# Third cross attention of a decoder: the folded weights' products in row halves of TensorE

## The chip, the cores and the metric

The kernel runs on one core of one Trainium2 chip, in one launch. The metric is device time in microseconds (us), the median of several executions. The profile is of one execution.

## The reference

A decoder of four layers, each with a self attention, a cross attention and a feed-forward part, each followed by a layer norm over 256 features: `x = layernorm(x + part(x))`. x is 8 sequences of 56 tokens, 448 tokens in all; the context has 8 x 1500 rows of 64 features. All is float32. The change is in the cross attention of layer 3, which is, cut to what matters:

```python
# 16 heads H, K = 128, D_CQ = 192, R = 64, D_C = 64
q_hk  = (hidden_q @ Wq.T).reshape(b, s, 16, 128)          # Wq: (2048, 256)
q_big = einsum('bshk,hkq->bshq', q_hk, w_kc_q)            # w_kc_q: (16, 128, 192)
kv_rope = rope(kv_c)
q_r = einsum('bshq,hqr->bhsr', q_big, W_qr)               # W_qr: (16, 192, 64)
k_r = einsum('bld,hdr->bhlr', kv_rope, W_kr)              # W_kr: (16, 64, 64)
scores = einsum('bhsr,bhlr->bhsl', q_r, k_r)
attn = softmax(scores)
ctx_c = einsum('bhsl,bld->bhsd', attn, kv_rope)           # then w_kc_kv and Wo
```

In this layer no rotation stands between q_hk and the scores (layers 0 and 2 have one on q_big), so all weights in front of the scores can be multiplied into one matrix for each head: scores = x . m3(h) . kv_rope, where m3 has 256 x 64 elements.

## The kernel before

The steps of `STEPS` run one after the other: self attention, cross attention and feed-forward of the four layers. `load` brings the weights of the next step in while a step runs: it issues DMAs on SyncE's queue (SP) into a pool of 16 buffers of 128 x 1024 elements, so a load starts when a buffer comes free. `xattn(3)` has two stages.

The first makes the folded weights and the queries. For each head, in this order:

- wqk = W_qr . W_kr, 192 x 64 (lines 691 to 702). The 192 rows are two parts ("halves") of 96. A matmul contracts over R = 64, so the even head of a pair uses rows 0 to 63 of TensorE's array and the odd head rows 64 to 127. These 32 matmuls go to the tile `ps_wqk`, one for each half, and are copied to SBUF by ScalarE (half 0) and VectorE (half 1).
- `turn_x` transposes the normed x to xT, 8 transposes into `ps_xT` and one copy by ScalarE.
- m2 = w_kc_q . wqk, 128 x 64 (lines 738 to 745): two matmuls of 96 rows for each head, added in `ps_m2`, and one copy of 128 x 1024 by VectorE.
- m3 = Wq . m2, two blocks c of 128 x 64 (lines 746 to 751): one matmul of 128 rows for each head and block into `ps_m3`, and one copy for each block, c = 0 by ScalarE and c = 1 by VectorE.
- qa = m3 . xT (`pair`, lines 718 to 732): the two heads of a pair go to the two halves of the columns of the array, ScalarE copies them from `ps_qk` to `qa`, and after each four heads two DMAs on ScalarE's queue copy qa to the other half of the partitions. `rows_of` issues the first context rows on the same queue.

PSUM is cut into two buffers of two banks (`bank2`: ps_wqk, ps_xT, ps_m2 and ps_m3 take them in turn) and three of one bank (`bank`: ps_qk). Profile rows leave the digit of a name out, so ps_m is ps_m2 and ps_m3, and m is m2 and m3; they tell apart by their inputs (l3x_c holds w_kc_q, l3x_q holds Wq, l3x_r and l3x_k hold W_qr and W_kr).

The second stage (`x_tiles`) walks over 56 tiles of queries with an order of instructions written out by hand: scores, exponent, transposes, weighted sum. It begins when qa is there.

Ahead of the stage the last token tile of the layer norm is finished on VectorE and ScalarE: `add` (lines 438 to 443), `rsqrt` (407 to 412) and `norm` (449). A scheduler orders the instructions of each engine where the code doesn't fix it; `self.mm(..., fixed=True)` and `self.ordered` fix it.

The matmuls of m2 in the code before:

```python
self.mm(
    ps[:, h // 8, (h % 8) * DC : (h % 8 + 1) * DC],
    [(kcq[h // 4][:, half, h % 4, :], wqk(half, h)) for half in range(2)],
)
```

Of the kernel before, what the change touches and what calls it, by code (L numbers as in the profile page):

```python
# [9 lines left out]
F32 = mybir.dt.float32  # L10
# [7 lines left out]
NB, S, D = 8, 56, 256  # L18
T = NB * S
TT = 112  # L20
NT = T // TT
L, DC = 1500, 64
# [98 lines left out]
def _rows(a):  # L121

    n = a.shape[0] // 128
    return a.reshape(n, 128, -1).transpose(1, 0, 2).reshape(128, -1)
# [14 lines left out]
def _groups(a, n):  # L139

    k, m = a.shape[0] // 128, a.shape[1]
    return a.reshape(k, 128, m // n, n).transpose(1, 2, 0, 3).reshape(128, -1)


def _pack(i):
    w = {}
# [4 lines left out]
    p = "L0_attn_"  # L151
# [6 lines left out]
    for n in (0, 2, 3):  # L158
        p = f"L{n}_xattn_"
        if n == 3:  # L160
            w[f"l{n}x_q"] = _rows(i[p + "Wq"])
            kcq = i[p + "w_kc_q"].transpose(2, 0, 1).reshape(2, 96, 4, 4 * 128)
            w[f"l{n}x_c"] = kcq.transpose(1, 2, 0, 3).reshape(96, -1)
        else:
            w[f"l{n}x_q"] = _groups(i[p + "Wq"].T, 512)
            w[f"l{n}x_c"] = i[p + "w_kc_q"].transpose(1, 0, 2).reshape(128, -1)

        for k, a in (("r", i[p + "W_qr"]), ("k", i[p + "W_kr"])):
            w[f"l{n}x_{k}"] = a.reshape(8, 2, -1, 64).transpose(1, 3, 0, 2).reshape(128, -1)
        w[f"l{n}x_o"] = _rows(i[p + "Wo"].T)  # L170
        w[f"l{n}x_v"] = i[p + "w_kc_kv"].transpose(1, 0, 2).reshape(128, -1)

    p = "L0_ffn_"
# [6 lines left out]
    p = "L1_attn_"  # L180
# [6 lines left out]
    p = "L1_xattn_"  # L187
# [5 lines left out]
    p = "L1_ffn_"  # L193
# [8 lines left out]
    p = "L2_attn_"  # L202
    q, kv = i[p + "q_w"], i[p + "kv_w"]
    k = np.repeat(kv[:64].reshape(4, 1, 16, D), 4, axis=1).reshape(D, D)
# [7 lines left out]
    p = "L2_ffn_"  # L212
# [8 lines left out]
    p = "L3_attn_"  # L221
# [15 lines left out]
    p = "L3_ffn_"  # L237
# [17 lines left out]
class Decoder:  # L255
# [420 lines left out]
    def xattn(self, n):  # L676
        nc, tc = self.nc, self.tc
        qrT, krT = self.rowsets(f"l{n}x_r", 192), self.rowsets(f"l{n}x_k", DC)
        kckv, wo = self.rowsets(f"l{n}x_v", DC), self.rowsets(f"l{n}x_o", D)

        with tc.tile_pool(name="xa", bufs=1) as outer:


            wm = outer.tile([128, 8, D], F32, name="wm")


            qa = outer.tile([128, NB * NQ], F32, name="qa")
            with tc.tile_pool(name="xq", bufs=2) as pool, self.psum(2, 3):

                wqk = pool.tile([128, 2, 16, DC], F32, bufs=1, name="wqk")  # L690
                at = lambda half, h: wqk[:96, half, h % 2 * 8 + h // 2]
                for half in range(2):
                    ps = self.bank2("ps_wqk")
                    for h in range(16):
                        j, rows = h // 2, slice(h % 2 * DC, (h % 2 + 1) * DC)
                        self.mm(
                            ps[:96, h % 2, j * DC : (j + 1) * DC],
                            [(qrT(j)[rows, half * 96 : (half + 1) * 96], krT(j)[rows])], fixed=True,
                        )
                    (nc.vector.tensor_copy if half else nc.scalar.copy)(  # L700
                        wqk[:96, half].rearrange("p (u h) d -> p u (h d)", u=2), ps[:96]
                    )
                self.turn_x(range(NT))
                context = self.x_context(outer)
                self.x_queries(n, pool, at, qa, context[2])
            with tc.tile_pool(name="xs", bufs=1) as pool, tc.tile_pool(name="psx", bufs=1, space=PSUM) as banks:
                self.x_tiles(pool, banks.tile([128, 8, 512], F32, name="ps_x"), qa, wm, kckv, wo, *context)

    def x_queries(self, n, pool, wqk, qa, rows_of):
        nc, xT = self.nc, self.xT  # L710

        def by_batch(a):
            return a.rearrange("p (b s) -> p b s", b=NB)

        flat = qa.rearrange("p (b o n) -> p b o n", b=NB, o=2)

        def pair(h, terms_of):


            ps = self.bank("ps_qk")  # L720
            terms = [terms_of(h + odd) for odd in range(2)]
            for k in range(2):
                for odd in range(2):
                    self.ordered(nc.tensor.matmul, ps[odd * DC : (odd + 1) * DC, :T], *terms[odd][k], start=k == 0, stop=k == 1)
            for odd in range(2):
                rows = slice(odd * DC, (odd + 1) * DC)
                nc.scalar.copy(flat[rows, :, odd, h // 2 * S : (h // 2 + 1) * S], by_batch(ps[rows, :T]))  # L727
            if h % 4 == 2:
                cols = slice((h // 2 - 1) * S, (h // 2 + 1) * S)
                for odd in range(2):  # L730
                    rows, others = (slice(u * DC, (u + 1) * DC) for u in (odd, 1 - odd))
                    nc.scalar.dma_start(flat[others, :, odd, cols], flat[rows, :, odd, cols])

        if n == 3:
            wq = self.rowsets(f"l{n}x_q", 256)
            kcq = [a.rearrange("p (q h k) -> p q h k", q=2, h=4) for a in self.parts(f"l{n}x_c")]

            m2 = pool.tile([128, 16, DC], F32, bufs=1, name="m2")
            ps = self.bank2("ps_m2")
            for h in range(16):  # L740
                self.mm(
                    ps[:, h // 8, (h % 8) * DC : (h % 8 + 1) * DC],
                    [(kcq[h // 4][:, half, h % 4, :], wqk(half, h)) for half in range(2)],
                )
            nc.vector.tensor_copy(m2.rearrange("p (u h) d -> p u (h d)", u=2), ps)
            m3 = pool.tile([128, 2, 16, DC], F32, bufs=1, name="m3")
            for c in range(2):
                ps = self.bank2("ps_m3")
                for h in range(16):
                    self.mm(ps[:, h // 8, (h % 8) * DC : (h % 8 + 1) * DC], [(wq(h)[:, c * 128 : (c + 1) * 128], m2[:, h, :])])  # L750
                (nc.vector.tensor_copy if c else nc.scalar.copy)(m3[:, c].rearrange("p (u h) d -> p u (h d)", u=2), ps)
            for h in range(0, 16, 2):
                if h and h % 4 == 0:
                    rows_of(0, h // 4 - 1)
                pair(h, lambda h: [(m3[:, c, h], xT[:, c, :]) for c in range(2)])
            return

        wq, kcq = self.heads(f"l{n}x_q"), self.rowsets(f"l{n}x_c", 192)

        def table(name):  # L760
            return self.const(name).rearrange("p (a s) -> p a s", a=2).unsqueeze(2).to_broadcast([96, 2, NB, S])

        cos, sin = table("xq_cos"), table("xq_sin")

        heads, ropes = {}, {}

        def projected(h):
            ps = self.bank("ps_qh")
            self.mm(ps[:, :T], [(wq(c, h), xT[:, c, :]) for c in range(2)], fixed=True)
            qh = heads[h] = pool.tile([128, T], F32, name="qh")  # L770
            nc.scalar.copy(qh, ps[:, :T])

        def rotated(h):
            qh = heads.pop(h)
            big = self.bank2("ps_big")
            for half in range(2):
                self.mm(big[:96, half, :T], [(kcq(h)[:, half * 96 : (half + 1) * 96], qh)], fixed=True)
            view = big[:96, :, :T].rearrange("p a (b s) -> p a b s", b=NB)
            rope = ropes[h] = pool.tile([96, 2, T], F32, bufs=5, name="rope")
            turn = pool.tile([96, 2, T], F32, name="turn")  # L780
            nc.vector.tensor_tensor(rope.rearrange("p a (b s) -> p a b s", b=NB), view, cos, ALU.mult)  # L781
            nc.vector.tensor_tensor(turn.rearrange("p a (b s) -> p a b s", b=NB), view, sin, ALU.mult)  # L782
            for half in range(2):
                nc.gpsimd.tensor_tensor(rope[:, half, :], rope[:, half, :], turn[:, 1 - half, :], ALU.add)  # L784


        for h in range(-3, 16):
            if h + 3 < 16:
                projected(h + 3)
            if 0 <= h + 2 < 16:  # L790
                rotated(h + 2)
            if h >= 0 and h % 2:
                if h % 4 == 3 and h < 12:
                    rows_of(0, h // 4)
                pair(h - 1, lambda h: [(wqk(half, h), ropes[h][:, half, :]) for half in range(2)])

    def x_context(self, pool):

# [1021 lines left out]
```

## Time and profile before

| what | value |
| --- | --- |
| median of 3 runs | 1674.08 us (1666.78 to 1682.12) |
| the profiled execution's own time | 1675.49 us |
| its span, first to last instruction | 1673.2 us |
| mean granted clock of TensorE | 0.922 |
| TensorE weight loads (PEld), busy | 904.6 us (54% of the span) |
| VectorE (DVE) busy | 1092.4 us (65%) |
| ScalarE (ACT) busy | 623.7 us (37%) |
| first stage of the third cross attention | from 1319.7 us (first wqk matmul) to 1372 us (last qa DMA issued) |
| in it: first matmul of m2, of m3, of qa | 1324.06, 1335.74, 1349.56 us |
| first qa DMA issued | 1354.55 us |

Times inside an execution are counted from the span's start. A row of the profile names the line, the engine, the operation, the tile written and the tiles read, the shape, and how often; for a matmul the shape is rows * columns of the stationary operand, then rows x columns of the moving one. PE is TensorE's multiplication, PEld its weight load, which overlaps it. One float32 matmul of the code shows as two records. The granted clock is the share of TensorE's clock that was allowed in a stretch. The chain of waits is followed back from the last instruction to what released each step; a time without a releaser is called issue.

### The profile page before, as it was taken

Reading aid. Unit: us, or ns where it says so; the run is one execution under the profiler, and the core shown is the slowest. Engines: PE = TensorE matmul, PEld = TensorE weight load, DVE = VectorE, ACT = ScalarE, POOL = GpSimd, SP = SyncE. Lnnn points to the kernel's source line nnn. Section 1 sums busy time; section 2 is a strip of 40 time slices with the busy share of each in tenths; the row PEclk is TensorE's granted clock in tenths of the full one; section 3 lists DMA queues with packets and bytes.
Section 4 is the critical chain, followed back from the end, with each engine's and each line's share of the span. In section 5 each row is a group of like instructions: output and inputs, shape, how many; then the busy total and the mean of one; then the engine's idle time right before and its main releaser. Section 6 shows DMA issues by size and latency. Waiting matters only on the chain.

```text
span 1673.2 us, 37625 instructions
## 1 busy us (share of the span) xinstructions
PE 1507.2 (90%) x16308; PEld 904.6 (54%) x16308; DVE 1092.4 (65%) x1787; ACT 623.7 (37%) x910; POOL 323.6 (19%) x302
## 2 busy tenths in 40 slices
PE   7989979999878678998979999899987988999998
PEld 4666435556544344654435556665655844555646
DVE  0575579999576764336579999436463219999743
ACT  2431245655212332103245556222443034665420
POOL 4711511212122010021511212101121000221200
PEclk9999979999997888999979999797997877999999
DMA  9523422323020001222422322012210452232100
GB/s 357 189 76 113 122 59 77 103 78 84 23 95 13 27 26 43 70 79 77 120 74 81 99 84 78 24 60 73 64 58 20 145 132 61 79 87 84 53 1 11
DMA packets 52103, 133.74 MB, mean 80 GB/s; under 512 B 20689, under 2 KB 21153, under 8 KB 51938
## 3 DMA queue, kind: packets, MB, share of 16 engines
q1 hardware_dynamic: 19922, 65.36, 12.0%
q10 hardware_dynamic: 28368, 50.25, 10.7%
q0 software_dynamic: 3648, 15.73, 2.9%
q8 instruction: 128, 2.10, 0.5%
q14 instruction: 37, 0.30, 0.1%
HBM read 119.06 MB, written 6.75 MB: 75 GB/s over the span
## 4 chain that ended last, share of the span: by engine, by line
PE 51%; DVE 9%; issue 7%; ACT 2%; DMA 1%; POOL 1%; ACTq 1%; DVEq 0%; POOLq 0%
PE ps_x L366 17%; PE ps_glu L358 8%; PE ps_y L358 7%; PE ps_qk L1628 2%; DVE sc L366 2%; PE ps_v L1628 2%; PE ps_qh L358 2%; PE ps_m L358 1%; PE ps_big L358 1%; PE ps_y L1628 1%; PE ps_q L358 1%; PE ps_qk L366 1%; PE ps_low L358 1%; PE ps_s L1350 1%; DVE E L1371 1%
## 5 line engine op out<-in xcount | busy, mean ns | idle before, releaser
L366 PE MATMUL ps_x<-kvT,qa 64*128 64x375 f32 x1344 | 308.1, 562 | 30.9 <-DVE sc L366 24.6
L366 ACT ACTIVATE sc<-sc,tops 128x1500 f32<-128x1500 f32 x168 | 259.2, 1543 | 150.1 <-DVE sc L366 115.6
L366 DVE STREAM_TRANSPOSE eT<-sc 128x1536 f32<-128x1536 f32 x168 | 296.9, 1767 | 11.5 <-PE ps_x L366 8.2
L366 PE MATMUL ps_x<-eT,kv 32*64 32x224 f32 x9024 | 256.5, 356 | 4.2 <-issue 3.9
L366 PEld LDWEIGHTS ps_x<-eT,kv 32*64 32x64 f32 x9024 | 196.8, 132 | 70.2 <-issue 60.4
L366 PEld LDWEIGHTS ps_x<-kvT,qa 64*128 64x128 f32 x1344 | 113.1, 199 | 187.7 <-DVE sc L366 161.5
L366 DVE TENSOR_SCALAR_CACHE_REDUCE sc<-ps_x 128x750 f32<-128x750 f32 x168 | 157.3, 936 | 38.9 <-PE ps_x L366 38.9
L366 DVE TENSOR_SCALAR_CACHE_REDUCE sc<-ps_x,tops 128x750 f32<-128x750 f32 x168 | 161.0, 958 | 1.2 <-PE ps_x L366 0.8
L366 POOL TENSOR_TENSOR eT<-eyes,sums 128x224 f32<-128x224 f32 x24 | 13.3, 554 | 452.2 <-DVE sums L366 452.2
L784 POOL TENSOR_TENSOR rope<-rope,turn 96x448 f32<-96x448 f32 x64 | 70.9, 1129 | 65.0 <-DVE turn L782 65.0
L781 DVE TENSOR_TENSOR rope<-ps_big,consts 96x896 f32<-96x896 f32 x32 | 34.8, 1086 | 58.4 <-PE ps_big L358 58.4
L1144 ACT ACTIVATE act<-ps_glu 128x448 f32<-128x448 f32 (+1 forms) x52 | 28.2, 543 | 111.1 <-PE ps_glu L358 107.8
L1148 DVE TENSOR_TENSOR act<-ps_glu,act 128x448 f32<-128x448 f32 x43 | 26.8, 624 | 65.2 <-ACT act L1144 65.1
L408 ACT ACTIVATE rstd<-rstd 112x3 f32<-112x3 f32 (+2 forms) x21 | 4.3, 204 | 166.5 <-DVE rstd L407 166.4
L614 DVE RECIPROCAL rec<-rec 128x896 f32<-128x896 f32 x8 | 46.0, 5753 | 26.7 <-ACT rec L613 26.7
L440 DVE TENSOR_TENSOR X<-X,ps_y 112x256 f32<-112x256 f32 x32 | 13.5, 421 | 70.6 <-PE ps_y L358 70.6
L366 PE MATMUL ps_x<-wm,qa 128*112 128x128 f32 (+1 forms) x336 | 49.0, 302 | 9.6 <-DVE qa L366 9.6
L1695 POOL TENSOR_TENSOR qk<-qk,sw 128x896 f32<-128x896 f32 x16 | 33.3, 2080 | 105.4 <-DVE sw L1694 105.4
L366 PEld LDWEIGHTS ps_x<-wm,qa 128*112 128x112 f32 x336 | 42.3, 182 | 20.1 <-issue 11.2
L727 ACT COPY qa<-ps_qk 64x448 f32<-64x448 f32 x48 | 25.3, 526 | 67.7 <-PE ps_qk L366 53.8
L366 POOL TENSOR_TENSOR qa<-num,rec 64x448 f32<-64x448 f32 x42 | 47.9, 1139 | 2.9
L1692 DVE TENSOR_TENSOR qk<-ps_qk,consts 128x896 f32<-128x896 f32 x16 | 17.5, 1092 | 33.4 <-ACT sw L1689 16.8
(411 smaller groups left out, 2447.3 us busy)
## 6 DMA issues: line engine op xcount, KB each, us to landing
kv<-kv ACTq DMA_DIRECT2D x288, 128.0 KB, 2.7
kvT<-kvT POOLq DMA_DIRECT2D x24, 384.0 KB, 3.6
qa<-qa ACTq DMA_DIRECT2D x24, 224.0 KB, 3.6
raw<-in_ctx ACTq DMA_DIRECT2D x6, 512.0 KB, 4.1
kv<-raw POOLq DMA_DIRECT2D x6, 512.0 KB, 4.0
kvT<-by POOLq DMA_DIRECT2D x6, 512.0 KB, 4.4
l0a_q<-in_l0a_q SPq DMA_DIRECT2D x4, 512.0 KB, 11.0
l0a_c<-in_l0a_c SPq DMA_DIRECT2D x4, 512.0 KB, 8.7
```

The lines of the kernel that those rows point to most:

```text
L358: ins = self.nc.tensor.matmul(out, lhsT, rhs, start=n == 0, stop=n == len(terms) - 1)
L366: call(*args, **kw)
L614: nc.vector.reciprocal(rec, rec)
L727: nc.scalar.copy(flat[rows, :, odd, h // 2 * S : (h // 2 + 1) * S], by_batch(ps[rows, :T]))
L781: nc.vector.tensor_tensor(rope.rearrange("p a (b s) -> p a b s", b=NB), view, cos, ALU.mult)
L784: nc.gpsimd.tensor_tensor(rope[:, half, :], rope[:, half, :], turn[:, 1 - half, :], ALU.add)
L1144: nc.scalar.activation(act, ps[:m, 0, :T], AF.Silu)
L1148: nc.vector.tensor_tensor(act, ps[:m, 1, :T], act, ALU.mult)
L1350: tc.keep_in_program_order(nc.tensor.matmul(*args, **kw))
L1628: tc.keep_in_program_order(nc.tensor.matmul(*args, **kw))
L1692: nc.vector.tensor_tensor(view(qk), view(ps[:, :, :T]), cos4, ALU.mult)
L1695: nc.gpsimd.tensor_tensor(qk, qk, sw, ALU.add)
```

## The change

Only the third cross attention changes; layers 0 and 2 keep their code (moved into `x_weights`, and `pair` into `pair_of`).

- The 192 rows of wqk become three parts of 64. A matmul is 64 rows by 64 columns, the even head in rows and columns 0 to 63 of the array and the odd head in 64 to 127: 48 matmuls, three `ps_wqk` tiles. wqk holds the even heads in partitions 0 to 63 and the odd ones in 64 to 127.
- m2 contracts over 64 rows, three times for each head, even and odd heads in turn in the two row halves, each to its own bank: 48 matmuls in two groups of four head pairs, each with its own `ps_m2`.
- m3 contracts over two 64 row blocks k of m2 for each head and c, even and odd heads in turn: 64 matmuls, two groups of four head pairs. A group has both blocks c.
- Every group is copied by ScalarE (even heads) and VectorE (odd heads): 6 copies of 64 x 512 for wqk (2 of 96 x 1024 before), 8 of 64 x 256 for m2 (1 of 128 x 1024), 4 of 128 x 512 for m3 (2 of 128 x 1024).
- m2 and m3 are in an order fixed by `ordered`. The arrays of w_kc_q and Wq come in another layout from the host: l3x_c is 3 tiles of 128 x 1024 instead of 4 of 96 x 1024, l3x_q stays 4 tiles.

```diff
-            w[f"l{n}x_q"] = _rows(i[p + "Wq"])
-            kcq = i[p + "w_kc_q"].transpose(2, 0, 1).reshape(2, 96, 4, 4 * 128)
-            w[f"l{n}x_c"] = kcq.transpose(1, 2, 0, 3).reshape(96, -1)
+            q = i[p + "Wq"].reshape(8, 2, 2, 64, D)
+            w[f"l{n}x_q"] = q.transpose(1, 3, 0, 2, 4).reshape(128, -1)
+            kcq = i[p + "w_kc_q"].reshape(8, 2, 128, 3, 64)
+            w[f"l{n}x_c"] = kcq.transpose(1, 4, 3, 0, 2).reshape(128, -1)
...
+    def x_weights3(self, pool, qrT, krT):
+        wqk = pool.tile([128, 3, 8, DC], F32, bufs=1, name="wqk")
+        for part in range(3):
+            ps = self.bank2("ps_wqk")
+            for j in range(8):
+                for odd in range(2):
+                    rows = slice(odd * DC, (odd + 1) * DC)
+                    self.mm(
+                        ps[rows, odd, j * DC : (j + 1) * DC],
+                        [(qrT(j)[rows, part * DC : (part + 1) * DC], krT(j)[rows])], fixed=True,
+                    )
+            self.by_parity(lambda rows, odd: (wqk[rows, part].rearrange("p j d -> p (j d)"), ps[rows, odd]))
+        return wqk
+
+    def by_parity(self, copy):
+        for odd, call in enumerate((self.nc.scalar.copy, self.nc.vector.tensor_copy)):
+            call(*copy(slice(odd * DC, (odd + 1) * DC), odd))
...
+    def x_queries3(self, n, pool, wqk, qa, rows_of):
...
+        m2 = pool.tile([128, 2, 8, DC], F32, bufs=1, name="m2")
+        for four in range(2):
+            ps = self.bank2("ps_m2")[:, :, : 4 * DC].rearrange("p u (j d) -> p u j d", d=DC)
+            for j in range(4 * four, 4 * four + 4):
+                for part in range(3):
+                    for odd, rows in enumerate(halves):
+                        self.ordered(
+                            self.nc.tensor.matmul, ps[:, odd, j % 4], kcq[part][rows, j, :], wqk[rows, part, j],
+                            start=part == 0, stop=part == 2,
+                        )
+            for k in range(2):
+                self.by_parity(lambda rows, odd: (m2[rows, k, 4 * four : 4 * four + 4], ps[halves[k], odd]))
+        m3 = pool.tile([128, 2, 8, 2, DC], F32, bufs=1, name="m3")
+        for four in range(2):
+            ps = self.bank2("ps_m3").rearrange("p u (j c d) -> p u j c d", c=2, d=DC)
+            for j in range(4 * four, 4 * four + 4):
+                for c in range(2):
+                    for k in range(2):
+                        for odd, rows in enumerate(halves):
+                            self.ordered(
+                                self.nc.tensor.matmul, ps[:, odd, j % 4, c],
+                                wq[j // 2][rows, j % 2, k, c * 128 : (c + 1) * 128], m2[rows, k, j],
+                                start=k == 0, stop=k == 1,
+                            )
+            self.by_parity(lambda rows, odd: (m3[:, odd, 4 * four : 4 * four + 4], ps[:, odd]))
```

More of the change, by code (lines that the diff above doesn't have):

```diff
@@ L688, in xattn @@
             with tc.tile_pool(name="xq", bufs=2) as pool, self.psum(2, 3):
[L690 to L702, printed above, removed]
+                rotary = n != 3
@@ L703, in xattn @@
+                wqk = (self.x_weights if rotary else self.x_weights3)(pool, qrT, krT)
                 self.turn_x(range(NT))
                 context = self.x_context(outer)
-                self.x_queries(n, pool, at, qa, context[2])
+                (self.x_queries if rotary else self.x_queries3)(n, pool, wqk, qa, context[2])
             with tc.tile_pool(name="xs", bufs=1) as pool, tc.tile_pool(name="psx", bufs=1, space=PSUM) as banks:
                 self.x_tiles(pool, banks.tile([128, 8, 512], F32, name="ps_x"), qa, wm, kckv, wo, *context)
-    def x_queries(self, n, pool, wqk, qa, rows_of):
[L710 to L756, printed above, removed]
@@ new lines, in x_weights @@
+    def x_weights(self, pool, qrT, krT):
+        nc = self.nc
+        wqk = pool.tile([128, 2, 16, DC], F32, bufs=1, name="wqk")
+        for half in range(2):
+            ps = self.bank2("ps_wqk")
+            for h in range(16):
+                j, rows = h // 2, slice(h % 2 * DC, (h % 2 + 1) * DC)
+                self.mm(
+                    ps[:96, h % 2, j * DC : (j + 1) * DC],
+                    [(qrT(j)[rows, half * 96 : (half + 1) * 96], krT(j)[rows])], fixed=True,
+                )
+            (nc.vector.tensor_copy if half else nc.scalar.copy)(
+                wqk[:96, half].rearrange("p (u h) d -> p u (h d)", u=2), ps[:96]
+            )
+        return lambda half, h: wqk[:96, half, h % 2 * 8 + h // 2]
@@ new lines, in x_weights3 @@
+    def x_weights3(self, pool, qrT, krT):
+        wqk = pool.tile([128, 3, 8, DC], F32, bufs=1, name="wqk")
+        for part in range(3):
+            ps = self.bank2("ps_wqk")
+            for j in range(8):
+                for odd in range(2):
+                    rows = slice(odd * DC, (odd + 1) * DC)
+                    self.mm(
+                        ps[rows, odd, j * DC : (j + 1) * DC],
[3 more added lines that the diff above has]
+        return wqk
@@ new lines, in by_parity, with pair_of @@
+    def by_parity(self, copy):
+        for odd, call in enumerate((self.nc.scalar.copy, self.nc.vector.tensor_copy)):
+            call(*copy(slice(odd * DC, (odd + 1) * DC), odd))
+    def pair_of(self, ps, qa, h, terms):
+        nc = self.nc
+        flat = qa.rearrange("p (b o n) -> p b o n", b=NB, o=2)
+        for k in range(2):
+            for odd in range(2):
+                self.ordered(nc.tensor.matmul, ps[odd * DC : (odd + 1) * DC, :T], *terms[odd][k], start=k == 0, stop=k == 1)
+        for odd in range(2):
+            rows = slice(odd * DC, (odd + 1) * DC)
+            nc.scalar.copy(flat[rows, :, odd, h // 2 * S : (h // 2 + 1) * S], ps[rows, :T].rearrange("p (b s) -> p b s", b=NB))
+        if h % 4 == 2:
+            cols = slice((h // 2 - 1) * S, (h // 2 + 1) * S)
+            for odd in range(2):
+                rows, others = (slice(u * DC, (u + 1) * DC) for u in (odd, 1 - odd))
+                nc.scalar.dma_start(flat[others, :, odd, cols], flat[rows, :, odd, cols])
@@ new lines, in x_queries3 @@
+    def x_queries3(self, n, pool, wqk, qa, rows_of):
+        xT = self.xT
+        kcq = [a.rearrange("p (j k) -> p j k", j=8) for a in self.parts(f"l{n}x_c")]
+        wq = [a.rearrange("p (j k m) -> p j k m", j=2, k=2) for a in self.parts(f"l{n}x_q")]
+        halves = [slice(odd * DC, (odd + 1) * DC) for odd in range(2)]
+        m2 = pool.tile([128, 2, 8, DC], F32, bufs=1, name="m2")
[7 more added lines that the diff above has]
+                            start=part == 0, stop=part == 2,
+                        )
+            for k in range(2):
[5 more added lines that the diff above has]
+                for c in range(2):
+                    for k in range(2):
+                        for odd, rows in enumerate(halves):
[3 more added lines that the diff above has]
+                                start=k == 0, stop=k == 1,
+                            )
+            self.by_parity(lambda rows, odd: (m3[:, odd, 4 * four : 4 * four + 4], ps[:, odd]))
+        for h in range(0, 16, 2):
+            if h and h % 4 == 0:
+                rows_of(0, h // 4 - 1)
+            self.pair_of(self.bank("ps_qk"), qa, h, [[(m3[:, odd, h // 2, c], xT[:, c, :]) for c in range(2)] for odd in range(2)])
@@ L758, in x_queries @@
+    def x_queries(self, n, pool, wqk, qa, rows_of):
+        xT, nc = self.xT, self.nc
         wq, kcq = self.heads(f"l{n}x_q"), self.rowsets(f"l{n}x_c", 192)
@@ L794, in x_queries @@
                     rows_of(0, h // 4)
-                pair(h - 1, lambda h: [(wqk(half, h), ropes[h][:, half, :]) for half in range(2)])
+                self.pair_of(
+                    self.bank("ps_qk"), qa, h - 1,
+                    [[(wqk(half, g), ropes[g][:, half, :]) for half in range(2)] for g in (h - 1, h)],
+                )
     def x_context(self, pool):
```

## The prediction

> **What bounds the kernel now.** I read the page first: TensorE is busy for most of the span, so an edit of matmuls can count, but only where they stand on the chain.
>
> ```profile
> PE 1507.2 (90%) x16308; PEld 904.6 (54%) x16308; DVE 1092.4 (65%) x1787; ACT 623.7 (37%) x910; POOL 323.6 (19%) x302
> ```
>
> Then the chain of waits in order of time, from 1300 to 1370 us (start, us, what):
>
> ```profile
> 1319.80 2.89 PE ps_wqk L358 x64
> ...
> 1322.78 1.23 DVE wqk L700
> 1324.02 0.04 issue
> 1324.06 10.32 PE ps_m L358 x64
> 1334.38 1.36 issue
> 1335.74 13.89 PE ps_m L358 x64
> 1349.63 4.34 PE ps_qk L366 x16
> ```
>
> The stage's three products stand end to end, nothing beside them. wqk costs 2.9 us, m2 10.3, m3 13.9, and 1.4 pass between m2 and m3 in the copy of m2. Next the instructions that touch ps_m and ps_wqk (duration min/median/max; the form is rows*columns of the stationary part, then rows x streamed columns):
>
> ```profile
> L358 PE MATMUL ps_m<-wqk,l3x_c x64: 275/275/421, 1324.1 to 1334.0; 96*128 96x64 f32 x64
> L358 PE MATMUL ps_m<-m,l3x_q x64: 421/421/443, 1335.7 to 1349.2; 128*128 128x64 f32 x64
> ```
>
> ```profile
> L358 PE MATMUL ps_wqk<-l3x_k,l3x_r x64: 245/245/293, 1319.7 to 1322.4; 64*96 64x64 f32 x64
> ```
>
> One matmul of the code is two records. m2 and m3 have the same 64 streamed columns and 64 records, yet m3 takes 3.6 us more. The busy times of 1 us stretches say why (PE busy and records, PEld, DVE, ACT, POOL, granted clock, DMA share, GB/s):
>
> ```profile
> 1326.00:1327.00 1.00, 1.00 (x11) 1.00 (x11) 0.00 (x0) 0.00 (x0) 0.00 (x0) 1.00 1.05 307
> 1328.00:1329.00 1.00, 1.00 (x7) 1.00 (x7) 0.00 (x0) 0.00 (x0) 0.00 (x0) 0.52 1.09 223
> 1347.00:1348.00 1.00, 1.00 (x7) 1.00 (x6) 0.00 (x0) 0.00 (x0) 0.00 (x0) 0.50 0.69 188
> 1352.00:1353.00 1.00, 1.00 (x8) 0.32 (x6) 0.00 (x0) 0.51 (x1) 0.00 (x0) 1.00 0.81 262
> ```
>
> Four microseconds into m2 the clock falls to a half and returns only in ps_qk, though PE was busy all along. From the starts of the records: one record per 112 ns at full clock, 213 at half. So 64 x 112 = 7.2 us is what either product costs at full clock; about 10 us of the stage are lost clock.
>
> [...] The trace agrees: all its clock stretches are multiples of 3.41 us and only 1.0 and 0.5 occur. [...] this trace shows it with PE busy. So I summed the matmul records of before by those windows, as share of array cells streamed: (rows x columns)/16384 x streaming time, where 448 columns take 376 ns and so 64 take 54. Below 0.37 the next window is at half, above at full: right for 404 of 407 windows at full clock and all 75 at half. m2 gives 0.75 x 54/112 = 0.36: it falls. m3 at full clock would give 0.48 and hold it, but at half it gives 0.25 and cannot regain it. [...] in wqk two records of the two row halves start 7 ns apart, one such pair per 85 ns, for 96 columns.
>
> **The change, part by part.** The price of a pair of 64x128 halves comes from the nearest row, 56x128 with 56 streamed columns, two halves as well. In order of time (the third attention's self attention; first at full clock, then at half):
>
> ```profile
> 1244.24 1.86 PEld L1628 LDWEIGHTS ps_y<-eT,V 56*128 56x128 f32 x32 [0.65 <-issue]
> ...
> 1275.78 3.49 PEld L1628 LDWEIGHTS ps_y<-eT,V 56*128 56x128 f32 x32 [0.99 <-ACT eT L1741]
> ```
>
> 16 pairs in 1.86 and 3.49 us; by starts 112 and 214 ns a pair. So:
> - m2: 48 matmuls, 96 records, 48 pairs: 5.4 us at full, 10.3 at half (before 10.3).
> - m3: 64 matmuls, 128 records, 64 pairs: 7.2 at full, 13.7 at half (before 13.9).
> - wqk: 48 matmuls of 64x64, 48 pairs. By the row 128*64 x 56 (59 ns a record) a pair costs 59 ns, 0.95 us a part, 2.8 in all. [...]
>
> The halves do twice the pairs of one record's work, so m3 gains nothing by packing; m2 a quarter. All else is clock, and what stands in front decides it.
>
> **What is late in front.** In the built order, each ACT/DVE pair of copies serialises: the DVE copy waits for the ACT copy of the same tiles, as V's copies do in before:
>
> ```profile
> L1709 DVE COPY V<-ps_v x4: 1228/1228/1228, 1170.3 to 1197.5; 56x1024 f32<-56x1024 f32 x4
> ...
>   ACT V L1708: 19.2, 4
> ```
>
> wqk copies go from 2 (1.0 ACT, 1.2 DVE) to 6 of 64x512: 0.58 (ACT, its 64x512 rows) and 0.70 (DVE, 56x512 row), 1.3 us a part. Two DVE ones come ahead of instructions of the last norm (rstd to X, 1320.97 to 1322.59 before); part 3 waits for bank pair 1, so for the DVE copy of part 1. Walking the order with these durations, 0.3 us from last matmul to copy: part 1 ends 1320.67, ACT copy 1321.0 to 1321.6, DVE to 1322.3, part 3 1322.4 to 1323.3; X of the last tile 1324.25 (+1.7); transposes end 1324.5; the third DVE copy ends 1325.0 and m2 starts 1325.05 instead of 1324.06: 1.0 us lost. PE idles some 0.7, 0.3 and 0.55 us in 1321.6 to 1325.05.
> Behind it nothing is late: m2's second half (2.7 us) covers the four copies of the first (0.37+0.42 twice, with hops 1.9 us; uncovered they would cost those 1.9), m3's halves (3.6) cover theirs and m3's first half its copies. So the 1.36 us between m2 and m3 goes, and ps_qk needs only m3's first half: the 1.1 us wait for DVE m goes too. DMAs: l3x_c is 3 tiles of 512 KB for 4 of 384, the same bytes; one tile fewer lets SP's queue run one buffer earlier. l3x_c is freed at m2's end for all tiles, so some l3f loads come up to 4 us later after m2 begins; their users are in the feed-forward stage 200 us on. Cost nothing; without that cover a late 512 KB load is 6.4 us (the page's row of l3f_g). New source layouts cost nothing, they are inputs.
>
> Is the clock kept over that front? Shares: wqk new 2 x 0.25 x 54/59 = 0.45 (before 0.47), transposes 0.65 us of cells in all, idle 0. A window that starts between about 1319.5 and 1322 averages 0.31 to 0.37: below. [...] I slid them over all phases: 62% lose the clock just before m2 or at its start; at 0.15 us more per hop, 90%. Once lost, m2 and m3 give 2 x 0.5 x 107/214 at half speed, 0.25: never regained before ps_qk. If kept, 0.48 holds it through both.
>
> **The cases.** Against the profiled execution (1675.49, span 1673.2), by the time of the first ps_qk:
> - A, clock lost at the front: m2 1325.1 to 1335.4, m3 to 1349.1 at half, before 1349.56; plus the 1.1 us stall gone: 1.5 gained.
> - B, clock kept: 5.4 + 7.2 from 1325.05 is 1337.6: 12.0; plus the stall and ps_qk's first microseconds at full clock: the first qa DMA at 1340.3 for 1354.55, 14.2 gained. The chain after it (copies and qa DMAs) is the same.
>
> **Rivals.**
> - B is the main rival. For it: shares of 0.48 in both products. Against: the idle front. It gives 1674.08 - 14.2 = 1659.9. It needs a front with under about 0.4 us idle.
> - C, slower: the halves don't fully overlap. At half clock the change breaks even at (1349.56 + 1.1 - 1325.1)/112 = 228 ns a pair; without any overlap a pair is 2 x 213 and the stage 23 us longer, about 1697; at 240 ns a 1.4 us loss, 1675.5. For it: no 64x64 or 64x128 pair of 64 columns is in the trace. Against: 214 for 56x128, 85 for 64x96.
> - D, no effect beyond the stage: m2 gains its quarter at full clock for the first window and nothing else; that is within A.
>
> **How the numbers follow.** Chances per execution: A 0.66, B 0.30, C 0.04. The time predicted is a median over executions whose phases differ (before they spread over 15 us), and in the likeliest case most are A's, some B's. With A at -1.5, B at -14.2 and 5 us of other spread, two to one, half of them lie below -4.5: 1674.08 - 4.5 = 1669.6. A's own range: 1664 to 1677. Range with B and the spread of few runs: 1657 to 1678. 1% is 16.7 us, about what a measurement of this kernel can tell from no change. Faster by over that needs B and 2.5 us of luck in the runs: 0.10. Slower: C at its worst, or luck: 0.05. Within: 0.85.
>
> **What would show it.** Right: ps_m of m2 as 96 records and m3 as 128, in pairs of 112 or 214 ns; m2's start about 1 us later after ps_y's end; ps_wqk in three groups with an idle gap; clock 0.5 in m2 and m3 (A) or 1.0 to their end (B); no issue gap before m3. Wrong: records of a pair not 7 ns apart; the clock falling inside m2 in spite of 0.48; a gap between m2's halves; qa's first DMA not earlier.

## The result and the profile after

The changed kernel takes 1666.09 us (median of 11 runs, 1656.41 to 1671.79) where the kernel before takes 1674.75 (11 runs beside it): ratio 0.9939, 95% interval 0.9918 to 0.996. Measured again later, on 10 runs, it is 0.9945 (0.9927 to 0.9963). So it is 0.6% faster: within the 1% that the prediction called "same", inside its range of 1657 to 1678, and 3.5 us under its point.

The profiled execution took 1661.03 us, span 1658.8. First the page's busy times:

```profile
PE 1491.6 (90%) x16436; PEld 895.2 (54%) x16436; DVE 1093.8 (66%) x1793; ACT 626.2 (38%) x917; POOL 323.6 (20%) x302
```

TensorE has 128 matmul records more than before, and PE is busy for 15.6 us less: the number of records didn't shrink, their pace changed. The chain of waits through the stage (start, us, what):

```profile
1315.39 1.10 PE ps_wqk L360 x32
...
1318.51 0.70 DVE wqk L734
...
1319.43 0.41 DVE X L451
...
1319.87 0.70 DVE wqk L734
...
1320.62 12.72 PE ps_m L368 x224
1333.35 3.18 PE ps_qk L368 x16
```

m2 and m3 are one piece of 12.7 us where before there were 10.3 + 1.4 + 13.9, and nothing stands between them. In front, the chain now runs through VectorE's copies of wqk and the last X of the norm. The rows of the products (duration min/median/max, first and last start, form), then those of wqk:

```profile
L368 PE MATMUL ps_m<-m,l3x_q x128: 272/272/272, 1326.0 to 1333.1; 64*128 64x64 f32 x128
...
L368 PE MATMUL ps_m<-wqk,l3x_c x96: 272/272/320, 1320.6 to 1325.9; 64*128 64x64 f32 x96
```

```profile
L360 PE MATMUL ps_wqk<-l3x_k,l3x_r x96: 218/218/267, 1315.3 to 1318.9; 64*64 64x64 f32 x96
```

The median is 272 ns in both products, where m3 had 421 before: all of it ran at full clock (1.00 in the rows of m2 and m3 below). By the starts of the records the two halves of a pair begin 7 ns apart and a pair takes 112 ns; a pair in wqk takes 59. The stretches of 1 us (PE busy and records, PEld, DVE, ACT, POOL, granted clock, DMA share, GB/s):

```profile
1317.00:1318.00 1.00, 0.45 (x16) 0.31 (x12) 0.77 (x2) 0.83 (x3) 0.13 (x1) 1.00 0.72 209
...
1322.00:1323.00 1.00, 1.00 (x22) 1.00 (x22) 0.00 (x0) 0.00 (x0) 0.00 (x0) 1.00 1.02 294
...
1332.00:1333.00 1.00, 1.00 (x23) 1.00 (x20) 0.00 (x0) 0.00 (x0) 0.00 (x0) 1.00 1.00 406
```

PE is idle for 1.0 us in all between the first wqk matmul and m2 (0.55, in the first of these rows, then 0.16 and 0.31), and yet the clock stays 1.0 in the middle of m2 and to the end of m3, where the kernel before shows 0.50. This execution is the prediction's case B.

Where did the time come from? The stage is measured from the first wqk matmul to the first qa DMA: 34.82 us before, 21.79 after, **13.0 us gained**. The profiled execution also came into the stage 4.4 us earlier (1315.3 for 1319.7), in code that is the same; the profiles of all kernels below come into it between 1312.8 and 1323.3, so that is no part of the change. Together 17.4, but the spans differ by 14.4. So about **3 us of this pair of profiles were lost again later**: from the last qa DMA to the end it is 300.7 us before and 303.6 after. The first scores stand level behind that DMA. The clock is at a half there until 3.3 us behind it before and until 6.0 after, and from 6 us on the scores after are 0.75 us later. Then comes this, in stretches of 5 us at equal distance from the DMA (30 to 40 us), first before:

```profile
1402.56:1407.56 5.00, 4.78 (x80) 2.92 (x88) 4.47 (x9) 2.93 (x3) 0.00 (x0) 0.60 0.18 67
1407.56:1412.56 5.00, 5.00 (x104) 2.65 (x88) 4.36 (x6) 1.93 (x4) 0.00 (x0) 1.00 0.01 3
```

and after:

```profile
1385.12:1390.12 5.00, 4.36 (x42) 2.16 (x48) 5.00 (x9) 2.18 (x3) 0.00 (x0) 0.50 0.29 82
1390.12:1395.12 5.00, 5.00 (x126) 3.37 (x112) 2.83 (x6) 1.09 (x2) 0.00 (x0) 0.82 0.00 0
```

The clock has fallen to a half for 17.1 us in both, 16.9 us behind the last qa DMA before and 19.7 after, and it comes back 34.0 us behind it before and 36.8 after. The scores behind it are 1.75 us later from there, and the rest is lost further on.

This is a difference of two profiles and not shown to be a cost of the change. From the last qa DMA to the end the code is the same in all kernels here, and it takes 300.7 to 306.7 us in their twelve profiles; in filled, with the same 13.0 us gained in the stage, it takes 300.9. For this pair, 13.0 less the loss behind it is 10.1 us; the medians give 8.7 and 9.0, the ratios 9 to 10.

### The profile page after: what moved, and what is told of

It is laid out like the page before. It is cut to its first block, busy times and chain, and to the rows that moved or that the text cites. A ratio compares the mean times of both kernels' runs of the same rounds, so it can differ in the third digit from the quotient of the medians.

```text
span 1658.8 us, 37891 instructions
## 1 busy us (share of the span) xinstructions
PE 1491.6 (90%) x16436; PEld 895.2 (54%) x16436; DVE 1093.8 (66%) x1793; ACT 626.2 (38%) x917; POOL 323.6 (20%) x302
## 4 chain that ended last, share of the span: by engine, by line
PE 50%; DVE 9%; issue 7%; ACT 2%; DMA 1%; ACTq 1%; POOL 1%; DVEq 0%; POOLq 0%
PE ps_x L368 18%; PE ps_glu L360 8%; PE ps_y L360 7%; PE ps_qk L1666 2%; DVE sc L368 2%; PE ps_v L1666 2%; PE ps_qh L360 2%; PE ps_big L360 1%; PE ps_y L1666 1%; PE ps_q L360 1%; PE ps_low L360 1%; PE ps_qk L368 1%; PE ps_m L368 1%; DVE E L1409 1%; DVE mx L1406 1%
## 5 line engine op out<-in xcount | busy, mean ns | idle before, releaser
L368 DVE STREAM_TRANSPOSE eT<-sc 128x1536 f32<-128x1536 f32 x168 | 296.9, 1767 | 11.3 <-PE ps_x L368 9.2
L368 PEld LDWEIGHTS ps_x<-wm,qa 128*112 128x112 f32 x336 | 43.4, 186 | 20.7 <-issue 11.2
```

Source lines behind the costliest of these rows:

```text
L368: call(*args, **kw)
```

## The experiments

Two theories. **Clock**: what halves TensorE's clock in the stage of before is the small share of array cells that its m2 streams (0.36), though PE is busy throughout; the change pays because its m2 streams 0.48 of the cells and because nothing interrupts it. **Halves and waits**: the gain comes from the packing into row halves and from the waits removed by smaller copies. In each run the stage is read from its own profile.

Shares of cells here are estimates, worked out as in the prediction from the shapes and starts of the matmul records: 64 columns are taken as 54 ns, from the 376 ns between records of 448 columns in before. A window is one step of 3.41 us of the recorded clock: in the traces of before and after every stretch of it is a multiple of that, but for the last, which the end of the profile cuts off.

**whole128**: the kernel before, its 192 rows cut into 128 and 64, the second part filled up with zeros to 128 rows (zero rows of w_kc_q); nothing is in halves.

```diff
-            kcq = i[p + "w_kc_q"].transpose(2, 0, 1).reshape(2, 96, 4, 4 * 128)
...
+            kcq = i[p + "w_kc_q"].transpose(2, 0, 1).reshape(192, 4, 4 * 128)
+            second = np.concatenate([np.zeros_like(kcq[:64]), kcq[128:]])
...
+                R, step = (128, 64) if n == 3 else (96, 96)
...
-                            [(qrT(j)[rows, half * 96 : (half + 1) * 96], krT(j)[rows])], fixed=True,
+                            [(qrT(j)[rows, half * step : half * step + R], krT(j)[rows])], fixed=True,
```

> The kernel before with one size changed: the 192 rows of wqk are taken as 128 and 64 (the second matmul of m2 also has 128 rows, 64 of them zero weights), so m2 has the same 64 records, one after the other, but with 128 rows instead of 96; nothing runs in row halves in m2 and m3. Clock theory (m2 of 96 rows streams 0.36 of the array's cells and so loses the clock, 128 rows stream 0.48 and keep it): clock 1.0 through m2 and m3 in most executions, both 64 records in 7.2 us instead of 10.3 and 13.9; wqk 0.9 us longer. From the first wqk matmul to the first qa DMA about 25 us instead of 34.8; median some 9 us below before, about 1665 to 1667. Packing theory (the gain of the change is the overlap of the two row halves): no gain, 0.9 us slower than before, about 1675, clock 0.5 from inside m2 as before.

Measured: 1672.37 us (22 runs), ratio 0.9987 (0.997 to 1.0003). The large gain did not come. The chain of waits says why:

```profile
1323.01 7.36 PE ps_m L359 x64
1330.37 1.36 issue
1331.73 12.10 PE ps_m L359 x64
```

m2 is at full clock (1.00 in the stretch from 1325 us), 7.4 us for 10.3: with 128 rows and 0.48 of the cells the clock holds here, as the theory has it. But m3, the same instructions, took 12.1, and the stretches (columns as above) show the clock falling behind the copy of m2:

```profile
1330.00:1331.00 1.00, 0.37 (x4) 0.23 (x3) 0.59 (x1) 0.00 (x0) 0.00 (x0) 1.00 0.92 360
...
1335.00:1336.00 1.00, 1.00 (x7) 1.00 (x6) 0.00 (x0) 0.00 (x0) 0.00 (x0) 0.50 0.00 0
```

The 1.36 us without matmuls bring the cell share of the window around them to about 0.29, an estimate from 0.48 of the cells in the other 2.05 of its 3.41 us. So what I had overlooked in this expectation is the second half of the change: the hidden copies are worth not 1.36 us but the clock of all of m3. The next pair of runs takes that apart.

**gapless128 and gapless96**: m2 and m3 as whole matmuls in two groups of eight heads, whose copies lie beside the next group; the first with the 128 rows of whole128, the second with the 96 rows of before. Between them only the number of rows differs (and with it the columns of the matmuls that make wqk, so that m2 starts 0.85 us later with 128).

```diff
+            for four in range(2):
+                ps = self.bank2("ps_m2")[:, :, : 4 * DC].rearrange("p u (j d) -> p u j d", d=DC)
+                for h in range(8 * four, 8 * four + 8):
+                    for half in range(2):
+                        self.ordered(
+                            nc.tensor.matmul, ps[:, h % 2, h // 2 % 4], kcq[h // 4][:, half, h % 4, :], wqk(half, h),
+                            start=half == 0, stop=half == 1,
+                        )
+                by_parity(lambda odd: (m2[:, 4 * four : 4 * four + 4, odd], ps[:, odd]))
```

> The kernel before with 192 rows as 128 and 64 (the second part filled up to 128 rows with zeros), nothing in row halves in m2 and m3, but m2 and m3 in two groups of eight heads whose copies by ScalarE and VectorE lie beside the next group's matmuls. Clock theory: the 128 row matmuls give a cell share of 0.48 and no copy interrupts them, so the clock stays 1.0 to the end of m3; m2 7.2 us and m3 7.2 us, first qa DMA about 23.5 us after the first wqk matmul (34.8 in the kernel before, 21.8 in the changed one); about 11 us less than before, 1665. Row-half theory (the halves themselves bring the gain): no gain but for the two waits, 2.5 us, so 1674.

> The same two groups with hidden copies, but m2 keeps its 96 rows in two parts and the layout of before. Clock theory: m2's cell share of 0.36 lets the clock fall within m2 as before, m3 runs at half; m2 about 10 us, m3 13.7; only the 1.36 us between m2 and m3 and the 1.1 us ahead of ps_qk go: first qa DMA 32 to 33 us after the first wqk matmul, 2 to 3 us less than before, 1674. Wait theory (the hidden copies, not the cells, keep the clock): clock 1.0 through both, 11 to 12 us less, as the run with 128 rows.

Measured: gapless128 1667.21 us (9 runs), ratio 0.9946 (0.9926 to 0.9966); gapless96 1675.17 (22 runs), 0.9999 (0.9983 to 1.0015). The chains, first of gapless128, then of gapless96:

```profile
1327.50 14.51 PE ps_m L367 x128
1342.00 3.18 PE ps_qk L367 x16
```

```profile
1324.29 23.95 PE ps_m L366 x128
1348.24 5.16 PE ps_qk L366 x16
```

128 records each, no gap in either, and 14.5 us against 24.0. Without a single row half in m2 and m3, gapless128 makes a gain that its interval can't tell from that of the change; without the cells, the hidden copies alone make none. The theory of halves and waits falls. In gapless128 64 of the 128 rows of the second part have zero weights; m2's share of the cells is 0.48 with them, and the clock stayed 1.00 (stretches from 1329, 1334 and 1340 us); it is 0.36 without, in gapless96, and the clock fell to 0.50 (1329 and 1340 us). Clock's figure of 11 us for gapless128 holds in the stage (first qa DMA 23.45 us after the first wqk matmul, 11.4 gained); the median is 8.0 lower than that of the kernel before beside it, the ratio stands for 9. For gapless96 it was too high: m3 begins 1.6 us earlier after the first wqk matmul than before (14.42 for 16.01), but the first qa DMA only 0.8 (34.01 for 34.82), as ps_qk takes 5.16 us there and took 4.34 before.

**fill96**: gapless96 with eight useless bf16 matmuls among those of m2.

```diff
+                    if h % 2 == 0:
+                        fill = self.bank("ps_fill")
+                        self.ordered(
+                            nc.tensor.matmul, fill[:, :T], self.idb,
+                            self.masks["m_before"].unsqueeze(1).to_broadcast([128, 8, S]), start=True, stop=True,
+                        )
```

> The kernel with m2 of 96 rows in two groups (hidden copies), which brought nothing (ratio 0.9999), plus one useless bf16 matmul of 128x128 with 448 columns (0.19 us each) ahead of each two heads of m2, eight in all, into a PSUM bank that nothing reads. Clock theory: per two heads 8 records of 112 ns with 0.36 of the cells and 0.19 us with all of them, a share of about 0.46; the clock stays 1.0 through m2 and m3, m2 takes 8.7 us and m3 7.2, first qa DMA about 24 us after the first wqk matmul instead of 34.0: about 10 us less than before, 1665 to 1667, although TensorE does more. If the halves or the waits make the gain and not the clock's count of cells: the clock falls in m2 as without the extra matmuls, and the time is that of before or 1.5 us more, 1675 to 1677.

Measured: 1667.34 us (9 runs), ratio 0.9944 (0.9925 to 0.9964). From its chain:

```profile
1325.91 0.19 PE ps_fill L366
1326.11 0.84 PE ps_m L366 x8
...
1332.29 7.99 PE ps_m L366 x72
1340.28 3.18 PE ps_qk L366 x16
```

One stretch of m2, first of gapless96, then of fill96:

```profile
1329.00:1330.00 1.00, 1.00 (x7) 1.00 (x6) 0.00 (x0) 0.00 (x0) 0.00 (x0) 0.50 0.93 340
```

```profile
1329.00:1330.00 1.00, 1.00 (x11) 1.00 (x10) 0.42 (x1) 0.37 (x1) 0.00 (x0) 1.00 1.01 264
```

m2 with its extra matmuls takes 8.3 us for 10.3, and m3 7.3 for 13.9: TensorE does more and is done 10.4 us earlier in the stage than in gapless96 (first qa DMA at 23.56 us). No count of PE's idle time explains this, as PE has none in m2 in either (1.00 busy in both rows).

**m2_only**: the changed kernel, m3 as 32 whole matmuls of 128 rows, for which the layout of m2 changes too (4 copies of 128 x 256 for 8 of 64 x 256).

```diff
-                    for k in range(2):
-                        for odd, rows in enumerate(halves):
...
-                                wq[j // 2][rows, j % 2, k, c * 128 : (c + 1) * 128], m2[rows, k, j],
...
+                    for odd in range(2):
...
+                            wq(2 * j + odd)[:, c * 128 : (c + 1) * 128], m2[:, j, odd], start=True, stop=True,
```

> The changed kernel with m3 again as one matmul of 128 rows for each head and block (32 matmuls, 64 records), m2 and wqk in row halves as changed. Clock theory: the same share of cells in m3 (0.48), so m3 takes 7.2 us at full clock as in the changed kernel, first wqk matmul to first qa DMA 21.8 us, median within 3 us of the changed kernel's 1666.1. Packing theory: m3 loses its overlap and its gain: 14 us instead of 7.3, about 1673.

Measured: 1660.84 us (6 runs), ratio 0.9913 (0.9883 to 0.9943); first qa DMA at 21.93 us, clock 1.0 through both. m3 takes the same 7.3 us with half as many records: packing m3 brings nothing, as the prediction's prices had it.

**late, filled and nudge** try the front of the changed kernel. late adds three VectorE copies of constants (128x1024); in its trace one runs ahead of X, one ahead of the last wqk copy and one behind it. nudge adds one of 128x512, which runs ahead of X. filled puts four bf16 matmuls into PE's idle time there.

```diff
+            if part == 2:
+                late = pool.tile([128, 1024], F32, bufs=1, name="late")
+                for _ in range(3):
+                    self.ordered(self.nc.vector.tensor_copy, late, self.C[:, :1024])
```

```diff
+            self.filler((0, 2, 1)[part])
...
+    def filler(self, n):
+        for _ in range(n):
+            ps = self.bank("ps_fill")
+            rhs = self.masks["m_before"].unsqueeze(1).to_broadcast([128, 8, S])
+            self.tc.keep_in_program_order(self.nc.tensor.matmul(ps[:, :T], self.idb, rhs, start=True, stop=True))
```

(the fourth stands behind the transposes of X, that is behind `turn_x`)

> The changed kernel with three copies of constants to an unused tile on VectorE (0.7 us each, two of them ahead of the last copy of wqk), so that TensorE waits some 1.4 us longer ahead of m2. Clock theory: the window ahead of m2 falls below 0.37 in every execution, m2 and m3 run at 0.5 and don't regain the clock: 10.3 and 13.7 us, first wqk matmul to first qa DMA 21.8 + 1.4 + about 12 = 35 us, median about 1676, no better than before. Packing theory: only the 1.4 us are added, about 1667.5, 23.2 us for the stretch.

> The changed kernel with four matmuls of bf16 constants (128x128 by 448 columns, 0.2 us each) into an unused PSUM bank, where TensorE waits ahead of m2: two ahead of the third part of wqk, one behind it, one behind the transposes. The output is not touched. Clock theory with the front as the cause of the changed kernel's spread: the clock is 1.0 through m2 and m3 in every execution, first wqk matmul to first qa DMA 21.8 to 22.2 us, median 3 to 6 us below the changed kernel's, 1660 to 1663. If the front costs the changed kernel nothing: the same as the changed kernel within 1 us, or slower by the 0.3 us that the fillers may delay the third part.

> The changed kernel with one VectorE copy of 128x512 constants (about 0.35 us) ahead of the last X of the norm, so that m2 starts some 0.35 us later. In the profiles so far the window ahead of m2 held a cell share of 0.375 or 0.363 (two positions of the windows against the first wqk matmul, 1.48 and 2.22 us after it) and kept the clock. Clock theory with a threshold near 0.36: the share falls to 0.33 or 0.31, the clock goes to a half through m2 and m3, and 0.35 us of copy cost about 12 us: 1673 to 1675, as with the three longer copies. If the front's idle time acts only by its own length: 0.4 us more than the changed kernel, 1663 to 1667.

Measured: late 1674.92 us (14 runs), ratio 0.9991 (0.997 to 1.0013); filled 1662.36 (10 runs), 0.9919 (0.9894 to 0.9944); nudge 1666.17 (7 runs), 0.9922 (0.9892 to 0.9953). The chain of late:

```profile
1318.72 0.60 DVE late L368
1319.33 0.34 DVE X L451
...
1321.11 22.53 PE ps_m L368 x224
```

and of nudge:

```profile
1327.36 0.34 DVE late L368
1327.69 0.32 DVE X L451
...
1328.80 12.72 PE ps_m L368 x224
```

late starts m2 1.2 us later against the first wqk matmul than the changed kernel, and that costs nearly all of the gain: the clock is a half in 20.7 of the 22.5 us. This is the prediction's case A, brought about by three copies: the first qa DMA comes at 34.36 us, 0.5 before that of the kernel before. In nudge the copy delayed m2 by 0.2 us only, and the clock stayed 1.0. My expectation failed: the window ahead of m2 held an estimated 0.35 of the cells, and I had taken the clock to be lost there. In late's trace too a window of an estimated 0.34 in front kept the clock, and only the next, of about 0.30, lost it (0.97 in the stretch from 1322 us, 0.50 from 1324), whereas m2 of before lost it at 0.36. (These sums move by 0.01 to 0.02 with the point within a record at which its columns are taken to stream; the order of the three holds at every point I took.) The windows that kept it hold wqk's 64x64 matmuls; why they kept it isn't shown.

In filled PE is idle for 0.19 us in front instead of 1.0, and the stage is the changed kernel's to 0.01 us. Its median lies in the range of its first expectation, but its interval overlaps with those of the changed kernel, so it doesn't show whether the idle front costs the changed kernel anything.

**split**: m2_only with even and odd heads of wqk's first and third part in two one-bank PSUM tiles.

```diff
-            ps = self.bank2("ps_wqk")
+            ps = self.bank2("ps_wqk") if part == 1 else None
+            out = [ps[:, odd] if ps is not None else self.bank("ps_wqk") for odd in range(2)]
```

> The changed kernel with whole 128-row matmuls for m3 and with the even and odd heads of wqk's first and third part in two PSUM tiles of one bank, so that ScalarE's and VectorE's copies of a part need not follow each other. Expected: wqk's 48 matmuls without a break of over 0.3 us, m2 about 4.3 us after the first wqk matmul instead of 5.3, clock 1.0 through m2 and m3 at any position of the windows; first qa DMA some 20.8 us after the first wqk matmul; 1660 to 1662, at or 1 us under the run with m3 whole alone. If the serial copies are set by something else than the shared tile: m2 at 5.3 as before and no difference.

Measured: 1659.02 us (8 runs), ratio 0.9925 (0.99 to 0.9951). From its chain:

```profile
1313.86 3.03 PE ps_wqk L359 x96
1316.89 0.92 PE ps_xT L461 x8
1317.81 12.85 PE ps_m L367 x160
```

The three parts of wqk run through, m2 starts 3.9 us after the first wqk matmul for 5.3, the first qa DMA at 20.56 us. In its trace VectorE's copy of the first part starts 0.2 us after ScalarE's and runs beside it; in the changed kernel it starts 0.6 us after it, when ScalarE's has ended. So the wait was that of the shared tile. The 1.4 us are not its alone: the third part also takes other PSUM buffers than before and no longer waits for the copies of the first (0.55 us in the changed kernel); no run takes the two apart. The stage is the shortest of all, and the kernel is faster than the one before; against the changed kernel, m2_only, filled and nudge the intervals overlap.

**after_2**: the changed kernel again.

> The changed kernel once more, unaltered, for another profile of it and more times. If the windows of the clock stand at the same one or two positions against the stage as in the ten profiles so far (the last window edge 1.2 to 1.9 us ahead of the first wqk matmul), the clock is 1.0 through m2 and m3 again and the median is 10 to 13 us under before, 1662 to 1665. If they fall at random, as the prediction took them to, the clock is lost in m2 in about 6 profiles of 10, and the median is 1666 to 1670.

Measured: 1666.98 us (10 runs), ratio 0.9945 (0.9927 to 0.9963); the profile has the clock at 1.0 through m2 and m3 and the first qa DMA at 21.79 us. The positions of the windows are those of the first expectation; the median lies in the range of the second, although the stage gained 13.0 us. In this profile it is 304.9 us from the last qa DMA to the end, for 300.7 before.

All of it in one table (times within the stage from the first wqk matmul of the profiled execution; clock at the end of m3):

| kernel | m2 starts | clock | first qa DMA | stage gain | ratio (95%) |
| --- | --- | --- | --- | --- | --- |
| before | 4.33 | 0.5 | 34.82 | | |
| changed | 5.31 | 1.0 | 21.79 | 13.0 | 0.9939 (0.9918 to 0.996) |
| changed, again | 5.31 | 1.0 | 21.79 | 13.0 | 0.9945 (0.9927 to 0.9963) |
| whole128 | 5.19 | 0.5 | 31.53 | 3.3 | 0.9987 (0.997 to 1.0003) |
| gapless96 | 4.33 | 0.5 | 34.01 | 0.8 | 0.9999 (0.9983 to 1.0015) |
| late | 6.47 | 0.5 | 34.36 | 0.5 | 0.9991 (0.997 to 1.0013) |
| gapless128 | 5.18 | 1.0 | 23.45 | 11.4 | 0.9946 (0.9926 to 0.9966) |
| fill96 | 4.33 | 1.0 | 23.56 | 11.3 | 0.9944 (0.9925 to 0.9964) |
| nudge | 5.51 | 1.0 | 22.00 | 12.8 | 0.9922 (0.9892 to 0.9953) |
| m2_only | 5.31 | 1.0 | 21.93 | 12.9 | 0.9913 (0.9883 to 0.9943) |
| filled | 5.31 | 1.0 | 21.79 | 13.0 | 0.9919 (0.9894 to 0.9944) |
| split | 3.88 | 1.0 | 20.56 | 14.3 | 0.9925 (0.99 to 0.9951) |

The kernels fall into two groups, and the clock in m3 is what parts them.

## Why the prediction was right, and where it was not

- **What bounds the stage: right.** Ten microseconds of m2 and m3 were lost clock, not lost work. gapless128 gets them without row halves, fill96 with extra matmuls, late loses them with the same matmuls.
- **The prices: right.** Pairs of 64x128 were taken as 112 ns and are 112; 64x64 as 59 and are 59. m2 was to take 5.4 us and takes 5.6 to its last end, m3 7.2 and takes 7.3. m3 gains nothing by packing (m2_only). Rival C, halves that don't overlap, is out: the two of a pair start 7 ns apart and a pair takes 112 ns. Rival D is out with case A.
- **The front: right.** m2 was to start 1.0 us later and starts 0.98 later. The serial copies are as walked. But PE is idle for 1.0 us in it, where 1.55 were forecast, and case B, which was said to need under about 0.4, came about all the same.
- **The gap between m2 and m3: right that it goes, too low in worth.** It was priced at its own 1.36 us. In whole128 it costs the clock of m3: 12.1 us for the 7.4 that the same number of records took in m2 at full clock.
- **The stall ahead of ps_qk: its worth was too high where the clock is lost.** The sum for case A counted 1.1 us for it. In gapless96 the wait is gone, and of the 1.6 us by which ps_qk started earlier half was lost again: ps_qk took 5.16 us, where it takes 3.18 at full clock (gapless128).
- **Whether the clock is kept: this step failed.** "I slid them over all phases: 62% lose the clock just before m2 or at its start." That all positions are equally likely was an assumption, which no trace showed. From it came two to one for case A and the point of 4.5 us under before. All four profiles with that front (the changed kernel twice, m2_only, nudge with 0.2 us more) kept the clock. The front itself was walked well: slid over the changed kernel's own records, the prediction's count, below 0.37, still loses the clock in two thirds of the positions. Two other parts of the step are shown wrong.
  - The positions aren't spread over 3.41 us: in twelve profiles the last window edge lies 1.77 to 1.95 us ahead of the first wqk matmul nine times (1.93 in before, 1.94 in after), and 1.19 to 1.20 three times. Both profiles of the changed kernel have the first place, where the window in question holds an estimated 0.38 of the cells; a window half a microsecond earlier or later would hold 0.33 to 0.35. That its two profiles stood there is luck as far as the prediction goes. The first stretch of the clock on record begins 17.3 us after the span's start in before and 16.3 in after, and 1300 us further on the two stand level to 0.01 us. What brings the work there isn't shown.
  - The prediction's 0.37 was too high for a window with wqk in it: m2_only kept the clock at an estimated 0.366 at most, nudge at 0.355 at most.
- **The rest of the program: not the same in the profiles.** "The chain after it (copies and qa DMAs) is the same" holds up to the last qa DMA, 18.0 us behind the first in both. Behind it the profiles differ by up to 6 us with the same code, and the sum had no term for that. Case B alone would have said 14.2 us less and 1659.9; measured are 13.0 in the stage, 10.1 with the loss behind it in one pair of profiles, 9 to 10 by the ratios.
- **What is luck in it.** The point came within 3.5 us because two errors have opposite signs: the chance of A was too high, and the median gained less than case B's stage. "Same within 1%" would have come true in case A and in case B alike (1.5 and 14.2 us, both under 16.7), so that it was right says nothing of the mechanism; the traces and the experiments do.
- **DMAs: no effect seen.** No run took them apart.

What stays open: of the changed kernel's 21 timed executions only the profiled ones have a trace, so it isn't shown whether a few others lose the clock in the stage, or why its ratios (0.9939, 0.9945) lie a little above those of filled, nudge, m2_only and split (0.9913 to 0.9925), which stand for 12.6 to 14.6 us, about what their stages gain. The intervals overlap.

## What to carry to other kernels

In this kernel PE's busy time did not tell what its matmuls cost: in before it was 1.00 in stretches of m2 and m3 with the clock at 0.52 and 0.50. Where a trace shows the same, look at the rows of those matmuls and at the gaps between them, and test both by a run. Here few rows (96 in m2 of before, 0.36 of the cells) and a gap of 1.36 us (whole128, about 0.29 of the window) each came ahead of a clock of 0.5 that held up to ps_qk; the matmuls of 64 columns and 128 rows come to an estimated 0.48 of the cells at full clock, with a record each 112 ns, and to 0.25 at half, with one each 213 ns. More rows with hidden copies (gapless128), or even useless matmuls (fill96), mended it: 1.00 through m2 and m3. Price a gap in such a stage by the clock that it loses, not by its length: in whole128 1.36 us without matmuls went with 12.1 us for m3, and m2's as many records took 7.4. Take the positions of the windows from several profiles rather than as random (two places in twelve profiles here), and expect part of a gain to be lost or won again behind the stage (about 3 us in this pair of profiles).

## What the runs showed of the hardware that was not expected

- TensorE at 100% busy falls to half clock within m2 with 96 rows (gapless96: 0.50 in the stretch from 1329 us, share of cells 0.36) and stays at full with the same matmuls and eight more of 0.19 us (fill96: 1.00 there; the share is about 0.50, an estimate from eight records of 0.75 x 54 ns and one of 190 in each 1030 ns).
- Summed by windows over the matmul records of before and after (streaming put 0.08 us behind a record's start), the estimated share of cells is below 0.37 ahead of 144 of the 145 windows at half clock and ahead of 11 of the 820 at full. PE's busy share does not part them: it was over 99% ahead of 27 of the 145. These are counts on two traces of this case.
- ScalarE's and VectorE's copies out of two halves of one PSUM tile follow each other (0.58 then 0.69 us in the changed kernel); out of two tiles those of the first part ran side by side (split). Whether the chip or the order that the program keeps between uses of a tile sets this isn't shown.
